# A two-layer graph attention kernel: layer 2's destination factors from broadcast rows on ScalarE instead of from products with stored masks

## The chip, the cores and the metric

The kernel runs on one core of a Trainium2 chip. The metric is the device time of one execution in microseconds. An execution taken by the profiler gives the profile and the trace; its own time stands beside its span.

## What is computed

The input is x (6250 nodes, 768 numbers each) and 100,000 edges from a source to a destination, sorted by destination; every node also has an edge to itself. In the reference, cut to what matters:

```python
def gat_conv(x, src, dst, W, a_src, a_dst, bias, heads):
    h = (x @ W).reshape(n, heads, -1)
    alpha_s = (h * a_src[None]).sum(-1)
    alpha_d = (h * a_dst[None]).sum(-1)
    e = leaky_relu(alpha_s[src] + alpha_d[dst], 0.2)
    e = exp(e - segment_max(e, dst)[dst])
    alpha = e / (segment_sum(e, dst)[dst] + 1e-16)
    return segment_sum(h[src] * alpha[:, :, None], dst).reshape(n, -1) + bias

h = maximum(layernorm(x), 0.0)
h = relu(gat_conv(h, src, dst, W1, a_src1, a_dst1, b1, heads=4))   # 4 x 64
h = relu(gat_conv(h, src, dst, W2, a_src2, a_dst2, b2, heads=1))   # 256
h = relu(h @ Wm1 + bm1)
out = x + (h @ Wm2 + bm2)
```

All of it is in float32.

## The kernel before

**Three stages.** The feature stage (from 0 to about 172 us in the trace) normalises x, multiplies with W1 and stores one row a node in a table in DRAM. Layer 1's edges run from there to about 1387, layer 2's from about 1442 (after a passage between the layers) to about 2560; the last node steps end at 2578.4.

**How the edges are tiled.** A tile is 128 edges. Two tiles are a pair, which is the unit of most instructions; a step `g` has two pairs (half-steps `2g` and `2g + 1`), a unit `u` has two steps (8 tiles, whose destinations lie near 64 nodes), and a block `t` has two units: 16 tiles and 128 nodes. There are 49 blocks, 98 units, 196 steps, 391 pairs and 782 tiles in a layer.

**What a tile goes through.** For each tile GpSimd (POOL) issues an indirect DMA (`gather`, L645) that brings the 128 source rows into a buffer `G`; 20 pair buffers go round. The softmax weight of an edge is exp(leaky(s + d)), with s from the source and d from the destination. Up to a factor that depends on the destination alone, which the division removes, it is max(exp(s), exp(0.2 s) rho) with rho = exp(-0.8 d). The rows of the table hold exp(s) and exp(0.2 s) (`powers`, L205). To bring rho to the edges, a mask (destination against partition, bf16, one per unit) is multiplied on TensorE with `win`, three bf16 parts of rho (`meet`, L691: 16 small products a block, into `e_ps`), and the parts are added (`join`, L699). In `pair`, VectorE takes the product and the maximum (L712, L715). For layer 1 it then scales the gathered rows (L724) and multiplies with a one-hot matrix `hot` (L673). For layer 2 it builds a weighted one-hot matrix `hw` of 128 x 128 instead, from `iota_ps`, the destination column and w (L719), which TensorE multiplies with the gathered rows (L736), summing in `o_ps`.

**Masks.** In layer 1, `make_mask` (L662) compares a broadcast row of destinations with the partition's number, and stores each mask to `mask_d` in DRAM (L664, 97 stores). In layer 2, `fetch_mask` (L617) brings them back (97 loads). Both go over SyncE's (SP's) DMA queue.

**Node steps.** When a unit's sum is done, VectorE adds it to the overlapping part of the unit before (`take_sum`, L753), ScalarE (ACT) copies quarters into place (L762), and each full block goes through its node steps. Those of layer 1 turn the block, apply relu (L918), multiply with W2, and write a row of the next table (L966 to L970). Those of layer 2 (`Node2.steps`) scale (L1066), turn (L912), relu (L918), multiply with Wm1 (L1075), relu (L1080), multiply with Wm2 (L1024, L1085), add x (L1089) and store.

**What sets the order.** The order on each engine is written out by hand (`manual_schedule`). Each engine works through its instructions in order, and waits on semaphores where data or a buffer isn't there. In layer 2, `UP_AT` says at which half-step a unit's sum is taken, and `STEPS_AT` at which half-steps a block's six node steps are placed: block t at 8t + 19 + 1, 2, 5, 8, 11 and 14. Gathers are placed eight steps (16 pairs) ahead of use.

**Between the layers.** `matched` prepares `win` and the own-edge weights (`prepare`, L557 to L594) and loads the weights of the last products. Some rows of layer 2's first tiles were gathered before all nodes were done, and are completed by products and an addition (`first_whole`, L303 and L305).

Of the kernel before, what the change touches and what calls it, by code (L numbers as in the profile page):

```python
# [10 lines left out]
F32 = mybir.dt.float32  # L11
# [42 lines left out]
SOON_AT = {2 * (8 * i + 11) + 1: i for i in range(len(SOON))}  # L54
SOON_FROM, SOON_HELD = min(SOON), 6
BARE = 8


UP_AT = {4 * u + 11: u for u in range(NU - 16)}
# [10 lines left out]
def kernel(  # L70
# [486 lines left out]
    def prepare(wk, layer, H):  # L557

        s, d = sd[layer][:, :, :H], sd[layer][:, :, H:]
        rho = wk.tile([P, NT, H], F32, name="rho")  # L560
        nc.scalar.activation(rho, d, AF.Exp, scale=SLOPE - 1.0)
        parts = wk.tile([P, NT, H, 3], BF16, name="parts")
        nc.vector.tensor_copy(parts[:, :, :, 0], rho)
        r1 = wk.tile([P, NT, H], F32, name="r1")
        nc.vector.tensor_sub(r1, rho, parts[:, :, :, 0])
        nc.vector.tensor_copy(parts[:, :, :, 1], r1)
        r2 = wk.tile([P, NT, H], F32, name="r2")
        nc.vector.tensor_sub(r2, r1, parts[:, :, :, 1])
        nc.vector.tensor_copy(parts[:, :, :, 2], r2)

        win = wk.tile([P, NG + 4, 3 * H], BF16, name="win")
        pv = parts.rearrange("p n h k -> p n (h k)").unsqueeze(2)
        for q in range(4):
            r = slice(32 * q, 32 * q + 32)
            to = win[r, q:q + NG].rearrange("p (n j) k -> p n j k", j=4)
            of = pv[r].to_broadcast([32, NT, 4, 3 * H])
            if q % 2:
                nc.scalar.activation(to, of, AF.Copy)
            else:
                nc.vector.tensor_copy(to, of)  # L580
        nc.vector.memset(win[64:96, 0:2], 0.0)
        nc.vector.memset(win[96:128, 0:3], 0.0)
        nc.vector.memset(win[0:32, NG:NG + 4], 0.0)
        e1 = wk.tile([P, NT, H], F32, name="e1")
        nc.scalar.activation(e1, s, AF.Exp)
        e2 = wk.tile([P, NT, H], F32, name="e2")
        nc.scalar.activation(e2, s, AF.Exp, scale=SLOPE)
        v = wk.tile([P, NT, H], F32, name="v")
        nc.vector.tensor_mul(v, e2, rho)
        own = wk.tile([P, NT, H], F32, name="own")  # L590
        nc.vector.tensor_max(own, v, e1)
        nc.vector.tensor_reduce(flags[:, layer - 1:layer], sd[layer].rearrange("p n k -> p (n k)"),
                                AX.X, ALU.max, apply_absolute_value=True)
        return SimpleNamespace(win=win, own=own)  # L594
# [14 lines left out]
            drow[r] = rowsp.tile([P, 16 * P], BF16, name="drow")  # L609
            nc.sync.dma_start(drow[r], bcast(dmod_d, 16 * P, r * 16 * P))  # L610

    def fetch_mask(u):

        if u < NU:
            b = (min(8 * u + 8, LAST) - 8 * u) * P
            mask[u] = maskp.tile([P, 8 * P], BF16, name="mask")
            nc.sync.dma_start(mask[u][:, :b], mask_d[u * P:(u + 1) * P, :b])  # L617

    def layer_edges(layer, H, node, pre, matched, pre_pool):

# [3 lines left out]
        with tc.tile_pool(name=f"eg{layer}", bufs=5) as eg, \  # L624
                tc.tile_pool(name=f"hw{layer}", bufs=10 if layer == 1 else 14) as hwp, \
                tc.tile_pool(name=f"sum{layer}", bufs=4) as sums, \
                tc.tile_pool(name=f"sm{layer}", bufs=4) as sm:
            G, hot, e_ps, o_ps = {}, {}, {}, {}

            def tiles(g):  # L630

# [33 lines left out]

            def make_hot(g):

# [14 lines left out]

            def meet(t):

                if t >= NT:
                    return
                e_ps[t] = ps.tile([P, 16, 6 * H], F32, name="e_ps", tag="e")
                for u, at, a, b in ranges(t):
                    m = mask.pop(u)
                    for k in range(a, b):  # L690
                        nc.tensor.matmul(e_ps[t][:, at + k, :3 * H], m[:, k * P:(k + 1) * P],  # L691
                                         pre.win[:, 2 * u + 2], start=True, stop=True)

            def join(t):
                if t >= NT:
                    return
                (_, _, a, _), (_, at, _, b) = ranges(t)
                T = slice(a, at + b)
                nc.vector.tensor_reduce(  # L699
                    e_ps[t][:, T, 3 * H:4 * H],  # L700
                    e_ps[t][:, T, :3 * H].rearrange("p t (h k) -> p t h k", k=3), AX.X, ALU.add)

            def pair(g, p):

                if 2 * p not in tiles(g):
                    return
                Gp = G.pop(TPG // 2 * g + p)
                e1, e2 = ((Gp[:, :, RW[1]:RW[1] + 4], Gp[:, :, RW[1] + 4:]) if layer == 1 else
                          (Gp[:, :, HID:HID + 1], Gp[:, :, HID + 2:]))
                at = TPG * (g % 4) + 2 * p  # L710
                rho, v, w = (e_ps[g // 4][:, at:at + 2, k * H:(k + 1) * H] for k in range(3, 6))
                nc.vector.tensor_mul(v, e2, rho)  # L712
# [14 lines left out]
                u = g // 2  # L727
                if u not in o_ps:
                    o_ps[u] = ps.tile([P, RW[layer]], F32, name="o_ps", tag="o", bufs=3)
                for t in range(2):  # L730
                    k = 2 * p + t
                    if layer == 2:
                        l, r = hw[:, t], Gp[:, t]
                    else:
                        l, r = hot[g][:, k], hw[:, t].rearrange("p h c -> p (h c)")
                    nc.tensor.matmul(o_ps[u], l, r[:, :RW[layer]], start=(g % 2 == 0 and k == 0),  # L736
                                     stop=(g % 2 == 1 and k == tiles(g)[-1]))
# [107 lines left out]
            for g in range(NG):  # L845
# [20 lines left out]
                if j == 0:  # L866
# [27 lines left out]
                if NG - 3 <= g < NG - 1:  # L894
                    stay_warm(3)
                hot.pop(g, None)
                if layer == 1 and g == NG - 6:
                    first_sources(2)
            if layer == 1:
                gather_up(NU - 1)  # L900
                advance(NG)
                stay_warm(4)
                for k in range(5):
                    fetch_mask(k)
            while late:
                advance(NG)
            at_end.clear()
# [14 lines left out]
    with tc.tile_pool(name="w2p", bufs=1) as wp, tc.tile_pool(name="wk2", bufs=2) as wk:  # L922
# [4 lines left out]
        class Node1:  # L927
# [17 lines left out]
            def steps(self, t, sum_, most=None, last=None):  # L945
# [32 lines left out]
    with tc.tile_pool(name="wmp", bufs=1) as wp, tc.tile_pool(name="x3", bufs=4) as xp, \  # L978
# [454 lines left out]
```

## Time and profile before

| | us |
|---|---|
| median of 3 runs | 2571.82 |
| lowest and highest | 2562.27, 2574.3 |
| the profiled execution | 2580.24 |
| its span | 2578.4 |

| engine | busy, us | share of the span | instructions |
|---|---|---|---|
| PE (TensorE products) | 1809.2 | 70% | 7727 |
| PEld (TensorE weight loads) | 1288.6 | 50% | 7729 |
| DVE (VectorE) | 1397.1 | 54% | 4195 |
| ACT (ScalarE) | 409.4 | 16% | 1273 |
| POOL (GpSimd) | 1523.6 | 59% | 1666 |

The mean clock granted to TensorE was 0.802 of full speed. The page's lines name engine, line of the kernel, what is written and read, how many, busy time and mean duration, and the idle time of the engine just before, with what ended it. "issue" is idle time in which the engine waited for nothing that the profile shows; "remote" is a release by something the trace doesn't name. A float32 product shows as two records, each with a weight load.

### The profile page before, as it was taken

To read this page: it belongs to the slowest core of one execution; us is meant where nothing else is said; L and a number is where in the kernel's file an instruction comes from. 1 tells how busy PE (TensorE), PEld (TensorE's weight loads), DVE (VectorE), ACT (ScalarE), POOL (GpSimd) and SP (SyncE) were. 2 spreads that over 40 slices of the span, in tenths; PEclk is the share of its full clock that TensorE was granted. 3 is DMA by queue.
4 is the path that set the end of the run, shared out by engine and by line. 5 is a ranking of instruction groups with operands and counts; after the bars stand their busy time and mean duration, and the time that the engine had idled before them with its cause. 6 is when DMAs were issued, how large, how long until landed. Compare 5 with 4: busy or idle time off the path is not lost.

```text
span 2578.4 us, 26497 instructions
## 1 busy us (share of the span) xinstructions
PE 1809.2 (70%) x7727; PEld 1288.6 (50%) x7729; DVE 1397.1 (54%) x4195; ACT 409.4 (16%) x1273; POOL 1523.6 (59%) x1666
## 2 busy tenths in 40 slices
PE   9944768867767777677675656676766766777677
PEld 7732546646545555555553434454444444454455
DVE  7733666666666676576565443444444444444444
ACT  6730011111111111111111011111111111111111
POOL 5366555565655655565554566666666666666661
PEclk9975878878878888887888768777778778877778
DMA  9994444545544544454434434445554555444442
GB/s 351 358 329 114 143 140 137 147 137 147 149 141 143 154 143 143 143 149 138 142 107 125 126 113 152 146 140 152 153 150 136 151 152 156 151 136 145 148 147 76
DMA packets 167328, 400.37 MB, mean 155 GB/s; under 512 B 36631, under 2 KB 54254, under 8 KB 167174
## 3 DMA queue, kind: packets, MB, share of 16 engines
q0 software_dynamic: 75072, 211.10, 29.9%
q1 hardware_dynamic: 90732, 185.99, 21.0%
q10 hardware_dynamic: 1370, 1.48, 0.2%
q8 instruction: 65, 1.06, 0.2%
q14 instruction: 89, 0.73, 0.1%
HBM read 333.87 MB, written 64.56 MB: 155 GB/s over the span
## 4 chain that ended last, share of the span: by engine, by line
PE 30%; issue 22%; DVE 21%; another core or an unknown queue 16%; POOL 4%; DMA 3%; ACT 1%; SPq 0%; DVEq 0%; POOLq 0%; ACTq 0%
PE o_ps L736 17%; PE y_ps L1085 4%; DVE hw L724 4%; POOL G L645 4%; DVE hot L673 4%; PE missing L389 3%; PE h_ps L447 3%; DVE e_ps L722 2%; DVE e_ps L712 2%; DVE hw L719 2%; DMA G<-table,src_i 2%; DVE acc L753 2%; DVE mask L662 1%; PE tp L1075 1%
## 5 line engine op out<-in xcount | busy, mean ns | idle before, releaser
L645 POOL DMA_INDIRECT G<-table,src_i x1507 | 1431.5, 950 | 874.1 <-issue 377.3
L736 PE MATMUL o_ps<-G,hw 128*128 128x258 f32 x1564 | 524.6, 463 | 225.5 <-issue 196.2
L736 PE MATMUL o_ps<-hw,hot 128*128 128x260 f32 x1564 | 504.6, 463 | 207.6 <-issue 128.8
L736 PEld LDWEIGHTS o_ps<-G,hw 128*128 128x128 f32 x1564 | 353.0, 232 | 368.8 <-issue 272.0
L736 PEld LDWEIGHTS o_ps<-hw,hot 128*128 128x128 f32 x1564 | 337.8, 227 | 347.2 <-issue 169.0
L762 ACT ACTIVATE sum<-acc 32x260 f32<-32x260 f32 (+1 forms) x384 | 160.0, 417 | 1421.8 <-DVE hw L724 631.8
L719 DVE TENSOR_SCALAR hw<-iota_ps,dcol,w 128x128 f32<-128x128 f32 x782 | 285.0, 406 | 15.4 <-DVE w L715 0.6
L724 DVE TENSOR_TENSOR hw<-G,e_ps 128x520 f32<-128x520 f32 x391 | 271.8, 695 | 22.5 <-DVE e_ps L722 6.3
L389 PE MATMUL missing<-kept,soon_hit 128*128 128x268 f32 x1028 | 251.4, 398 | 35.2 <-issue 35.2
L379 DVE TENSOR_TENSOR soon_hit<-soon_of,iota_ps 128x1408 f32<-128x1408 int32 (+18 forms) x46 | 75.6, 1643 | 323.2 <-remote 258.8
L389 PEld LDWEIGHTS missing<-kept,soon_hit 128*128 128x128 f32 x1028 | 196.3, 195 | 75.2 <-issue 41.4
L1089 DVE TENSOR_TENSOR y<-y_ps,xt 128x384 f32<-128x384 f32 (+1 forms) x98 | 54.6, 557 | 289.8 <-PE o_ps L736 106.8
L1085 PE MATMUL y_ps<-wm,mT 128*128 128x384 f32 x392 | 182.0, 594 | 18.2 <-issue 15.5
L691 PE MATMUL e_ps<-win,mask 128*128 128x12 bf16 (+1 forms) x1564 | 72.0, 168 | 130.9 <-issue 122.6
L447 PE MATMUL h_ps<-w,r 128*128 128x264 f32 (+1 forms) x588 | 139.3, 390 | 9.6 <-ACT r L437 5.0
L691 PEld LDWEIGHTS <-mask 128*128 128x128 bf16 x1564 | 65.0, 100 | 148.0 <-issue 140.3
L673 DVE TENSOR_TENSOR hot<-iota_ps,dcol 128x512 f32<-128x512 f32 x196 | 133.6, 682 | 2.3 <-remote 2.3
L712 DVE TENSOR_TENSOR e_ps<-G,e_ps 128x8 f32<-128x8 f32 (+1 forms) x782 | 125.5, 160 | 5.2 <-issue 0.9
L1085 PEld LDWEIGHTS y_ps<-wm,mT 128*128 128x128 f32 x392 | 77.4, 219 | 98.4 <-issue 65.5
L447 PEld LDWEIGHTS h_ps<-w,r 128*128 128x128 f32 x588 | 108.8, 192 | 32.6 <-issue 7.2
L1080 ACT ACTIVATE mT<-tp,bm1c 128x128 f32<-128x128 f32 x98 | 30.6, 363 | 507.8 <-remote 235.1
L753 DVE SCALAR_TENSOR_TENSOR acc<-acc,keep,o_ps 128x260 f32<-128x260 f32 (+1 forms) x192 | 91.6, 477 | 14.3 <-PE o_ps L736 10.2
(415 smaller groups left out, 1246.8 us busy)
## 6 DMA issues: line engine op xcount, KB each, us to landing
xt<-in_x SPq DMA_DIRECT2D x96, 384.0 KB
drow<-dmod_d SPq DMA_DIRECT2D x49, 512.0 KB
mask_d<-mask SPq DMA_DIRECT2D x97, 256.0 KB
mask<-mask_d SPq DMA_DIRECT2D x97, 256.0 KB
G<-table,src_i POOLq DMA_INDIRECT x1507
xTt<-in_xT SPq DMA_DIRECT2D x49, 384.0 KB
out<-y SPq DMA_DIRECT2D x48, 384.0 KB
table<-kept SPq DMA_DIRECT2D x49, 134.0 KB
```

What stands on the lines that cost most here:

```text
L389: nc.tensor.matmul(soon_p[k], hit[:, T - there], kept[T], start=(T == there), stop=(T == NT - 1))
L447: nc.tensor.matmul(h_ps[:, :n], r[:, k], w1[:, k, :n], start=(k == 0), stop=(k == KI - 1))
L645: nc.gpsimd.indirect_dma_start(out=G[k // 2][:, k % 2], out_offset=None, in_=table[layer], in_offset=bass.IndirectOffsetOnAxis(ap=src_i[:, ...
L673: nc.vector.tensor_tensor(hot[g][:, T[0]:T[0] + n], iota_ps.unsqueeze(1).to_broadcast([P, n, P]), dcol[:, k:k + n].unsqueeze(2).to_broadca ...
L691: nc.tensor.matmul(e_ps[t][:, at + k, :3 * H], m[:, k * P:(k + 1) * P], pre.win[:, 2 * u + 2], start=True, stop=True)
L712: nc.vector.tensor_mul(v, e2, rho)
L719: nc.vector.tensor_scalar(hw[:, t], iota_ps, dcol[:, k:k + 1], w[:, t], ALU.is_equal, ALU.mult)
L724: nc.vector.tensor_mul(hw, Gp[:, :, :RW[1]].rearrange("p t (h c) -> p t h c", h=H), w.unsqueeze(3).to_broadcast([P, 2, H, C + 1]))
L736: nc.tensor.matmul(o_ps[u], l, r[:, :RW[layer]], start=(g % 2 == 0 and k == 0), stop=(g % 2 == 1 and k == tiles(g)[-1]))
L753: nc.vector.scalar_tensor_tensor(acc, run[0], keep[:, u % 2:u % 2 + 1], o_ps.pop(u), ALU.mult, ALU.add)
L762: nc.scalar.activation(done[t][r], acc[r], AF.Copy)
L1085: nc.tensor.matmul(y_ps, mT[:, j], wm2[:, j, s * half:(s + 1) * half], start=False, stop=(j == KH - 1))
```

## The change

Layer 2 no longer uses masks and products for its destination factors. The rows of layer 2's table hold s and -0.8 s instead of powers. `slopes` makes, for each unit, a row of 128 numbers -0.8 d, one for each destination of its window: copies on ScalarE, one transpose on TensorE, a copy, and a store to `slope_d`. It is called once in layer 1 at step 150 for units 0 to 55, and once at the start of layer 2 for the rest. `fetch_slopes` brings the rows of eight units at a time to all 128 partitions (up to 512 KB each, 13 loads on SP's queue, two buffers). In `pair`, ScalarE computes for each tile Relu(row - 0.8 s) and then Exp(that + s), each over 128 x 128 with a bias from the gathered row; VectorE's product and maximum of layer 2 go, and `hw` becomes (iota == destination) times this 128 x 128 weight. Layer 1 keeps its masks, products and joins, but no longer stores the masks. `prepare` no longer makes `win` for layer 2. The scratch for the descriptors of POOL's DMAs is halved.

```diff
+SLOPES, SLOPES_AT = 56, 150
...
-    mask_d = dram.tile([NU * P, 8 * P], BF16, name="mask_d")
+    slope_d = dram.tile([NU, P], F32, name="slope_d")
...
+        win = None
+        if layer == 1:
+            parts = wk.tile([P, NT, H, 3], BF16, name="parts")
...
-    def fetch_mask(u):
-
-        if u < NU:
-            b = (min(8 * u + 8, LAST) - 8 * u) * P
-            mask[u] = maskp.tile([P, 8 * P], BF16, name="mask")
-            nc.sync.dma_start(mask[u][:, :b], mask_d[u * P:(u + 1) * P, :b])
+    def slopes(pool, a, b):
+
+        n = b - a
+        rr = pool.tile([P, n + 2], F32, name=f"slope{a}")
+        nc.vector.memset(rr, 0.0)
+        for q, first, past in ((0, 0, 1), (1, 0, 0), (2, 0, 0), (3, -1, 0)):
+            lo, hi = max(a // 2 + first, 0), min(b // 2 + past, NT)
+            at = 2 * lo + (-1, 0, 0, 1)[q] - a + 1
+            r = slice(32 * q, 32 * q + 32)
+            nc.scalar.activation(rr[r, at:at + 2 * (hi - lo)].rearrange("p (n k) -> p n k", k=2),
+                                 sd[2][r, lo:hi, 1:2].to_broadcast([32, hi - lo, 2]), AF.Copy,
+                                 scale=SLOPE - 1.0)
+        p = ps.tile([P, P], F32, name="slope_ps", tag="e")
+        nc.tensor.transpose(p[:n], rr[:, 1:n + 1], ident)
+        turned = pool.tile([P, P], F32, name=f"slopeT{a}")
+        nc.scalar.activation(turned[:n], p[:n], AF.Copy)
+        nc.sync.dma_start(slope_d[a:b], turned[:n])
...
+            def fetch_slopes(k):
+
+                if layer == 2 and k * 8 < NU:
+                    n = min(8, NU - 8 * k) * P
+                    slope[k] = eg.tile([P, 8 * P], F32, name="slope", bufs=2)
+                    nc.sync.dma_start(slope[k][:, :n], bcast(slope_d, n, k * 8 * P))
...
                 if layer == 2:
-                    return fetch_mask(u + 1)
+                    return
...
-                nc.sync.dma_start(mask_d[u * P:(u + 1) * P, a:b], mask[u][:, a:b])
...
-                if t >= NT:
+                if t >= NT or layer == 2:
                     return
                 e_ps[t] = ps.tile([P, 16, 6 * H], F32, name="e_ps", tag="e")
...
                 if layer == 2:
-                    w = sm.tile([P, 2, H], F32, name="w")
-                    nc.vector.tensor_max(w, v, e1)
+                    u = g // 2
+                    rows = slope[u // 8][:, u % 8 * P:(u % 8 + 1) * P]
+                    w = sm.tile([P, 2, P], F32, name="w")
+                    for t in range(2):
+                        nc.scalar.activation(w[:, t], rows, AF.Relu, bias=Gp[:, t, HID + 2:])
+                    for t in range(2):
+                        nc.scalar.activation(w[:, t], w[:, t], AF.Exp, bias=Gp[:, t, HID:HID + 1])
                     hw = hwp.tile([P, 2, P], F32, name="hw")
                     for t in range(2):
                         k = TPG * g + 2 * p + t
-                        nc.vector.tensor_scalar(hw[:, t], iota_ps, dcol[:, k:k + 1], w[:, t],
-                                                ALU.is_equal, ALU.mult)
+                        nc.vector.scalar_tensor_tensor(hw[:, t], iota_ps, dcol[:, k:k + 1], w[:, t],
+                                                       ALU.is_equal, ALU.mult)
...
+            fetch_slopes(0)
             matched()
...
                     meet(t + 1)
+                    if t % 4 == 1:
+                        fetch_slopes(t // 4 + 1)
...
+                if layer == 1 and g == SLOPES_AT:
+                    slopes(pre_pool, 0, SLOPES)
...
-                for k in range(5):
-                    fetch_mask(k)
...
-                nc.scalar.activation(row[:, :HID], h_ps[:, :HID], AF.Copy)
-                powers(row[:, HID:HID + 1], row[:, HID + 2:], h_ps[:, HID:HID + 1])
+                nc.scalar.activation(row[:, :HID + 1], h_ps[:, :HID + 1], AF.Copy)
+                nc.scalar.activation(row[:, HID + 2:], h_ps[:, HID:HID + 1], AF.Copy, scale=SLOPE - 1.0)
...
+            slopes(pre, SLOPES, NU)
             vars(pre2).update(vars(prepare(pre, 2, 1)))
...
-                   dynamic_dma_scratch_size=8192)
+                   dynamic_dma_scratch_size=4096)
```

More of the change, by code (lines that the diff above doesn't have):

```diff
@@ L561, in prepare @@
         nc.scalar.activation(rho, d, AF.Exp, scale=SLOPE - 1.0)
[L562 to L583, printed above, removed]
+        win = None
+        if layer == 1:
+            parts = wk.tile([P, NT, H, 3], BF16, name="parts")
+            nc.vector.tensor_copy(parts[:, :, :, 0], rho)
+            r1 = wk.tile([P, NT, H], F32, name="r1")
+            nc.vector.tensor_sub(r1, rho, parts[:, :, :, 0])
+            nc.vector.tensor_copy(parts[:, :, :, 1], r1)
+            r2 = wk.tile([P, NT, H], F32, name="r2")
+            nc.vector.tensor_sub(r2, r1, parts[:, :, :, 1])
+            nc.vector.tensor_copy(parts[:, :, :, 2], r2)
+            win = wk.tile([P, NG + 4, 3 * H], BF16, name="win")
+            pv = parts.rearrange("p n h k -> p n (h k)").unsqueeze(2)
+            for q in range(4):
+                r = slice(32 * q, 32 * q + 32)
+                to = win[r, q:q + NG].rearrange("p (n j) k -> p n j k", j=4)
+                of = pv[r].to_broadcast([32, NT, 4, 3 * H])
+                if q % 2:
+                    nc.scalar.activation(to, of, AF.Copy)
+                else:
+                    nc.vector.tensor_copy(to, of)
+            nc.vector.memset(win[64:96, 0:2], 0.0)
+            nc.vector.memset(win[96:128, 0:3], 0.0)
+            nc.vector.memset(win[0:32, NG:NG + 4], 0.0)
         e1 = wk.tile([P, NT, H], F32, name="e1")
@@ L610, in fetch_rows @@
             nc.sync.dma_start(drow[r], bcast(dmod_d, 16 * P, r * 16 * P))
-    def fetch_mask(u):
-        if u < NU:
-            b = (min(8 * u + 8, LAST) - 8 * u) * P
-            mask[u] = maskp.tile([P, 8 * P], BF16, name="mask")
-            nc.sync.dma_start(mask[u][:, :b], mask_d[u * P:(u + 1) * P, :b])
+    def slopes(pool, a, b):
[5 more added lines that the diff above has]
+            at = 2 * lo + (-1, 0, 0, 1)[q] - a + 1
+            r = slice(32 * q, 32 * q + 32)
+            nc.scalar.activation(rr[r, at:at + 2 * (hi - lo)].rearrange("p (n k) -> p n k", k=2),
[6 more added lines that the diff above has]
+        nc.sync.dma_start(slope_d[a:b], turned[:n])
     def layer_edges(layer, H, node, pre, matched, pre_pool):
@@ L627, in layer_edges @@
                 tc.tile_pool(name=f"sm{layer}", bufs=4) as sm:
-            G, hot, e_ps, o_ps = {}, {}, {}, {}
+            G, hot, e_ps, o_ps, slope = {}, {}, {}, {}, {}
+            def fetch_slopes(k):
[3 more added lines that the diff above has]
+                    nc.sync.dma_start(slope[k][:, :n], bcast(slope_d, n, k * 8 * P))
             def tiles(g):
@@ L694, in join @@
             def join(t):
-                if t >= NT:
+                if t >= NT or layer == 2:
                     return
@@ L707, in pair @@
                 Gp = G.pop(TPG // 2 * g + p)
[L708 to L712, printed above, removed]
-                if layer == 2:
-                    w = sm.tile([P, 2, H], F32, name="w")
-                    nc.vector.tensor_max(w, v, e1)
+                if layer == 2:
+                    u = g // 2
[5 more added lines that the diff above has]
+                        nc.scalar.activation(w[:, t], w[:, t], AF.Exp, bias=Gp[:, t, HID:HID + 1])
                     hw = hwp.tile([P, 2, P], F32, name="hw")
@@ L718, in pair @@
                         k = TPG * g + 2 * p + t
-                        nc.vector.tensor_scalar(hw[:, t], iota_ps, dcol[:, k:k + 1], w[:, t],
-                                                ALU.is_equal, ALU.mult)
-                else:
+                        nc.vector.scalar_tensor_tensor(hw[:, t], iota_ps, dcol[:, k:k + 1], w[:, t],
+                                                       ALU.is_equal, ALU.mult)
+                else:
+                    e1, e2 = Gp[:, :, RW[1]:RW[1] + 4], Gp[:, :, RW[1] + 4:]
+                    at = TPG * (g % 4) + 2 * p
+                    rho, v, w = (e_ps[g // 4][:, at:at + 2, k * H:(k + 1) * H] for k in range(3, 6))
+                    nc.vector.tensor_mul(v, e2, rho)
                     nc.vector.tensor_max(w, v, e1)
```

## The prediction

> **What bounds the kernel now.** The whole page first: the shares of the engines, and the chain that ended last.
>
> ```profile
> PE 1809.2 (70%) x7727; PEld 1288.6 (50%) x7729; DVE 1397.1 (54%) x4195; ACT 409.4 (16%) x1273; POOL 1523.6 (59%) x1666
> ...
> PE 30%; issue 22%; DVE 21%; another core or an unknown queue 16%; POOL 4%; DMA 3%; ACT 1%; SPq 0%; DVEq 0%; POOLq 0%; ACTq 0%
> ```
>
> No engine is full, and a fifth of the chain is "issue", where the engine waits for nothing that the profile shows. ACT is at 16%. Averages hide stages, so next comes the table of busy time by stretch (us, then PE, PEld, DVE, ACT, POOL with their counts, granted clock, DMA share, GB/s). Layer 2's edges run from 1442 to about 2560.
>
> ```profile
> 1600.00:1800.00 200.00, 136.50 (x555) 91.69 (x555) 84.13 (x319) 29.34 (x77) 129.05 (x136) 0.75 0.48 143
> 1800.00:2000.00 200.00, 138.74 (x597) 95.05 (x597) 90.05 (x342) 28.83 (x76) 131.29 (x138) 0.77 0.49 146
> 2000.00:2200.00 200.00, 141.30 (x566) 91.58 (x566) 88.08 (x334) 29.39 (x77) 129.25 (x136) 0.77 0.50 149
> ```
>
> PE is busiest, at about 70%, and POOL's gathers come next; DVE is at 44%, ACT at 15%, DMA at half. Layer 2 takes (2560 - 1442) / 49 = 22.8 us for each block of 128 nodes (16 tiles of 128 edges, 8 pairs). Now the waits between 1500 and 2400 (total us, times, longest).
>
> ```profile
> PEld o_ps L736 <- issue: 238.7, 216, 2.7
> ACT mT L1080 <- remote: 210.0, 16, 19.3
> PE o_ps L736 <- issue: 169.7, 166, 2.7
> ...
> POOL G L645 <- issue: 157.2, 515, 0.6
> ...
> POOL G L645 <- remote: 72.2, 37, 3.7
> POOL G L645 <- PE o_ps L736: 61.1, 46, 3.6
> ```
>
> PE's edge product loses 170 us to "issue", not to a gather or a weight. POOL does wait for PE, some 3.6 us at a time: its ring of 20 pair buffers is full, and it goes on when PE frees a pair. So PE sets the pace of layer 2 and POOL follows. How close is POOL? Its order of time, from 1988:
>
> ```profile
> 1988.30 0.95 POOL L645 DMA_INDIRECT G<-table,src_i  x1 [0.30 <-issue]
> 1989.55 0.94 POOL L645 DMA_INDIRECT G<-table,src_i  x1 [0.30 <-issue]
> ...
> 1998.28 0.94 POOL L645 DMA_INDIRECT G<-table,src_i  x1 [0.30 <-issue]
> 2001.93 0.94 POOL L645 DMA_INDIRECT G<-table,src_i  x1 [2.71 <-remote]
> ```
>
> Unhindered it issues one gather per 1.25 us (0.95 and 0.30), which is 16 x 1.25 = 20.0 us a block: only 2.8 us below the 22.8. Last, PE in order of time around one run of the small products:
>
> ```profile
> 2035.74 1.90 PE L736 MATMUL o_ps<-G,hw 128*128 128x258 f32 x8
> 2037.48 1.05 PE L1075 MATMUL tp<-rT,wm 128*128 128x128 f32 x8
> 2038.37 0.54 PE L691 MATMUL e_ps<-win,mask 128*128 128x3 bf16 x16
> 2038.77 0.68 PE L736 MATMUL o_ps<-G,hw 128*128 128x258 f32 x2
> 2039.94 0.46 PE L736 MATMUL o_ps<-G,hw 128*128 128x258 f32 x1 [0.49 <-issue]
> 2042.04 0.38 PE L736 MATMUL o_ps<-G,hw 128*128 128x258 f32 x1 [1.64 <-issue]
> 2042.78 0.38 PE L736 MATMUL o_ps<-G,hw 128*128 128x258 f32 x1 [0.36 <-issue]
> ```
>
> Undisturbed, eight records (four tiles) take 1.74 us from start to start. Right after the 16 products of L691 PE falls into a halting stretch: single records 0.7 to 2 us apart with nothing waited for, about 12 us here (to 2052), and at the half clock afterwards. Undisturbed a block would need 16 x 0.435 = 7.0 for the edges, 2 x 1.66 for y, 0.9 and 0.2 for the two other products and 0.4 for L691: 11.8 us. The other 11 of the 22.8 us are halts and half clock. In order of time, most of these stretches in layer 2 begin within 2 us of an L691 run. None is seen from 0 to 172 us, where there is no L691, nor from 1344 to 1442, nor after 2494, when the last mask transfers leave SP's queue (one at 2500). Two of the last L691 runs (2509, 2533) are followed by none, so masks may matter rather than the products.
>
> **What the skill says.** "TensorE: Matmul & The Clock Gate", Part 1: the clock is either half or full, by activity in a window of about 3.4 us. The trace agrees: clock 0.75 to 0.77 as a mean, the same products at 0.22 or 0.46 us a record. "DMA: Bandwidth & Descriptors", Anatomy of one DMA (SWDGE): about 2.0 us fixed for a transfer started by POOL; here gathers land 2.1 to 2.3 us after issue, some 45 us ahead of use. "ScalarE: Activation LUTs", What ACT_TABLE_LOAD costs: 280 ns + 0.833 ns a column with a pointer bias, and neighbours overlap by about 93 ns. The trace agrees: L420 (one column, pointer bias, SBUF) 282 ns.
>
> **The change, part by part.**
> 1. Products with masks in layer 2 (784 of L691), and join (49 x 0.21 us of DVE), go. Between 1450 and 2400, 41 blocks, L691 is busy 27.0 us with 23.7 idle before it: 1.2 us a block. If halts belong to it or to its masks, up to 11 us a block go; but from 2.8 us on POOL is late, so that this is the most that a block gives in the long run.
> 2. The mask stores of layer 1 (97) and fetches of layer 2 (97 of 256 KB) leave SP's queue. Bounds: nothing (DMA is half used) to the halts of layer 1, about 340 us by adding them up in its order of time. I take nothing for layer 1, whose products stay.
> 3. DVE per pair: 0.157 (L712) and 0.160 (L715) go; the two hw instructions change from 406 ns to a two-tensor form. Nearest row: L753, 477 ns for 258 columns; less 130 columns at 1.05 ns (L1007: 784 columns in 976 ns; L1089: 384 in 557) gives 0.34; I take 0.34 to 0.41. DVE falls to about 8 us a block beside POOL's 20: worth nothing by itself.
> 4. ACT gains four 128-column instructions a pair, 1564 in all. From L420: 282 + 127 x 0.833 = 388 ns each, the pitch 0.29 to 0.39. A block: 32 x 0.29 to 0.39 = 9.4 to 12.4, plus now 29 us in 200 = 3.3: 13 to 16 us, under 20. The worst bound, L1066's 509 ns for 256 columns, would give 19.6. The hiding work is POOL's; without it 32 x 0.39 would bound. No table load is expected: L109's one serves Exp and Relu already.
> 5. A new order: ACT now stands between gather and hw. In its queue w of the next pair lies behind rT, mT, o and sum. mT waits for PE's m_ps of three half-steps before, so w is at most three pairs ahead. From m_ps to the hw needed: mT 0.62, w 1.5, hw 0.7, 2.8 us; PE's three pairs at POOL's pace are 7.5 us. Nothing; at PE's full pace (2.6) it would be tight. A gather's buffer is now held for ACT too, which is done with it before PE.
> 6. Slope rows: ACT copies, one transpose and a store twice; at step 150 the inputs are some six blocks old, at layer 2's start they cost 2 to 3 us, against 3 us of DVE and 1.4 of ACT (L578) that prepare loses. Zero net, under the fixes of L305, which hold the first pair until 1441.5. Slope fetches: 13 of 512 KB on SP against 97 of 256 KB; first needed long after issue. Rows with raw s instead of powers: one small ACT instruction fewer a block.
> 7. The smaller ring for descriptors: two to four gathers are in flight at 1.25 us and 2.3 us landing. Zero, at worst a new wait on POOL, which then counts fully.
>
> **The sum.** If the halts go with L691 and masks, POOL sets layer 2. In the trace 40 gathers of its 771 are started before 1456; the ring frees at 1444.4, and 741 more steps of 1.2547 us (its mean where it doesn't wait) end at 2374. Behind the last: landing 2.3, weights and last products about 2.5, and the last node steps, 15.5 from 2563 to 2578.4: 20 us. Span 2394. With the 1.84 around it 2396, against 2580.2 for the profiled execution; that stood 0.33% above the median of 2571.8, so 2388. I add 12 for waits of POOL while PE still catches up: 2400, a gain of 172.
>
> **Rivals.**
> - PE still halts, by time or by number of instructions. For it: layer 1's stretches don't always begin at L691. Against: the undisturbed end. Then only L691's own time goes: 1.2 to 2 us a block, 60 to 100 us: 2474 to 2514; say 2485.
> - Layer 1 gains as well, because mask traffic causes the halts: a third of its 340 us more, 2400 - 110 = 2290. For it: the stretches end with the masks. Against: one stretch a block, two masks.
> - ACT becomes the bound: slower. Place: the four instructions ahead of every hw. It decides from (22.8 - 3.3) / 32 = 0.61 us each with their waits; at 0.7, 25.7 us a block give 49 x 2.9 = 142 more: 2714. For it: ACT is strictly in order and w waits behind mT, whose waits reach 19 us now. Against: 0.39.
> - No change: another hidden limit, as the POOL wait of part 7, takes the 2.8 us: 2570.
>
> **Chances.** POOL-bound 0.50; halts stay 0.27; layer 1 too 0.07; ACT 0.11; no change 0.05. A difference of 0.5% is about what a measurement of this kernel can tell from none. Faster 0.84, same 0.05, slower 0.11. The range 2370 to 2560 leaves out ACT and layer 1, and takes in the bounds of the unknown costs.
>
> **What would show it.** Right: POOL's gathers at 1.25 us with hardly a wait for PE; PE waiting for DMA or hw; clock and "issue" changed in layer 2; layer 1 within 1% in length; ACT at some 15 us a block. Wrong: "issue" ahead of L736's successor undiminished; POOL still waiting for PE or now for ACT; ACT instructions of 0.6 us or more; layer 1 shorter.

## The result, and the profile after

| | before | after |
|---|---|---|
| median of 19 runs each, us | 2568.38 | 2582.47 |
| lowest and highest | 2562.27, 2575.78 | 2568.23, 2590.17 |
| the profiled execution | 2580.24 | 2584.67 |
| its span | 2578.4 | 2582.9 |

The ratio is 1.0055, with a 95% interval of 1.0043 to 1.0066: 14 us slower, where 172 us faster was forecast. The experiments ran in five groups, each beside the kernel before; in three of them (those of b_lean, a_narrow2 and a_copy2 below) the kernel before took 2099.8 to 2104.4 us instead of 2566.8 to 2591.0, no trace of those groups shows PE halting, and since what makes the difference was not found, every run is compared with before in its own group only.

The page of the changed kernel, its engines and its chain:

```profile
PE 1720.1 (67%) x6948; PEld 1236.2 (48%) x6949; DVE 1243.6 (48%) x3356; ACT 866.0 (34%) x2796; POOL 1524.2 (59%) x1666
...
another core or an unknown queue 6%; ACT 6%; PE 5%; DVE 2%; issue 2%; POOL 0%; DMA 0%
...
L739 DVE SCALAR_TENSOR_TENSOR hw<-iota_ps,dcol,w 128x128 f32<-128x128 f32 x782 | 245.4, 349 | 448.4 <-ACT w L735 291.5
...
L733 ACT ACTIVATE w<-slope,G 128x128 f32<-128x128 f32 x782 | 266.8, 389 | 48.6 <-issue 39.9
```

PE lost 89 us of work and DVE 153, ACT gained 457. POOL is as it was. The shares of the chain add up to a fifth only: the trace could not follow it. The table of busy time by stretch (columns as before):

```profile
1600.00:1800.00 200.00, 123.19 (x424) 82.79 (x423) 60.39 (x184) 108.12 (x348) 128.95 (x137) 0.78 0.44 130
1800.00:2000.00 200.00, 120.27 (x456) 84.83 (x454) 60.23 (x184) 108.90 (x351) 131.92 (x139) 0.81 0.45 129
2000.00:2200.00 200.00, 129.39 (x456) 85.21 (x456) 64.76 (x196) 110.42 (x355) 129.10 (x137) 0.81 0.46 134
```

PE's busy time was 136 to 141 us in 200 before and is some 124 now, and the number of gathers is the same 137. Work left the engines and the pace did not change: from the starts of the edge product, 40 blocks apart, a block takes 23.54 us before and 23.40 after. (The count starts at the fifth block. Started up to three blocks earlier or later it gives 23.33 to 23.56 before and 23.39 to 23.82 after, so the two don't differ.) Layer 1's last edge product starts at 1383.6 and 1383.5, and layer 2's first one at 1443.0 and 1442.3. The waits of the changed kernel between 1500 and 2400 (us, times, longest):

```profile
ACT mT L1108 <- remote: 251.0, 29, 21.3
PEld o_ps L760 <- DVE hw L739: 250.3, 44, 25.8
DVE y L1117 <- remote: 234.2, 25, 12.3
PE o_ps L760 <- DVE hw L739: 231.9, 29, 25.7
DVE hw L739 <- ACT w L735: 219.2, 89, 14.2
POOL G L666 <- issue: 146.1, 424, 3.6
POOL G L666 <- ACT mT L1108: 101.2, 29, 4.5
```

PE's "issue" is gone from the head of the list. In its place PE waits some 8 us at a time for hw, DVE waits 10 us at a time for "remote" before it adds x, and ACT for "remote" before mT. One block, on PE, then DVE, then POOL, in order of time:

```profile
2011.89 1.56 PE L1113 MATMUL y_ps<-wm,mT 128*128 128x384 f32 x4
2013.29 1.90 PE L760 MATMUL o_ps<-G,hw 128*128 128x258 f32 x8
2015.03 1.05 PE L1103 MATMUL tp<-rT,wm 128*128 128x128 f32 x8
2015.92 1.04 PE L760 MATMUL o_ps<-G,hw 128*128 128x258 f32 x4
2025.87 3.81 PE L760 MATMUL o_ps<-G,hw 128*128 128x258 f32 x8 [8.91 <-DMA G<-table,src_i]
```

```profile
2014.31 0.64 DVE L739 SCALAR_TENSOR_TENSOR hw<-iota_ps,dcol,w 128x128 f32<-128x128 f32 x2 [1.03 <-ACT w L733]
2024.99 0.56 DVE L1117 TENSOR_TENSOR y<-y_ps,xt 128x384 f32<-128x384 f32 x1 [10.04 <-remote]
2025.47 0.86 DVE L739 SCALAR_TENSOR_TENSOR hw<-iota_ps,dcol,w 128x128 f32<-128x128 f32 x3
```

```profile
2022.00 0.95 POOL L666 DMA_INDIRECT G<-table,src_i  x1 [0.30 <-issue]
2023.25 0.95 POOL L666 DMA_INDIRECT G<-table,src_i  x1 [0.30 <-issue]
2027.88 0.94 POOL L666 DMA_INDIRECT G<-table,src_i  x1 [3.68 <-ACT mT L1108]
```

DVE's second addition of y needs PE's products of L1113 and the loaded x. The products ran from 2011.89 to about 2013.4 (the ends of PE's records are modelled), and PE went on through 20 further records. The addition started only at 2024.99. The trace's own record of PE's signals (the semaphore updates by which other engines learn that a product is done; the trace has 1240 of PE's 1518) says why: none between 2016.56 and 2024.97, one more at 2027.11, and then seven in 0.35 us. By its records PE had done the work, but its signals came some 11 us late. All that waits for PE then waits: DVE's addition, hw behind it, mT, and PE itself for hw. (At 2025.87 the profile names a DMA as what PE waited for, but the hw that PE needs ended only at 2025.8.) POOL meanwhile goes on, until it has no free buffer, at 2024.20. I call this a hold.

Two more counts from the trace say what is late. Of the 75 additions of y between 1500 and 2400, 30 begin more than 2 us after both PE's products and DVE's own work before them were over; 29 of these begin 0.02 us after a signal of PE, so they don't wait for x. The signals of the other engines are hardly ever late: of 610 tiles in the same stretch, hw begins more than 0.5 us after its w and DVE's own work before it in 4, and PE's product never more than 0.06 us after its hw and PE's own work before it. In the profile before, the halting stretch that the prediction shows from 2039 to 2052 has the same signature: PE signals at 2041.33, 2044.17 and 2047.00, then nothing until 2054.12, then ten signals in 0.47 us. I take the halts before and the late signals after for the same thing.

### The profile page after: what moved, and what is told of

Same layout as the page of the kernel before. It is cut to its first block, busy times and chain, and to the rows that moved or that the text cites. A ratio compares the mean times of both kernels' runs of the same rounds, so it can differ in the third digit from the quotient of the medians.

```text
span 2582.9 us, 24782 instructions
## 1 busy us (share of the span) xinstructions
PE 1720.1 (67%) x6948; PEld 1236.2 (48%) x6949; DVE 1243.6 (48%) x3356; ACT 866.0 (34%) x2796; POOL 1524.2 (59%) x1666
## 5 line engine op out<-in xcount | busy, mean ns | idle before, releaser
L760 PE MATMUL o_ps<-G,hw 128*128 128x258 f32 x1564 | 471.2, 445 | 313.3 <-DVE hw L739 272.5
L760 PE MATMUL o_ps<-hw,hot 128*128 128x260 f32 x1564 | 496.5, 456 | 192.9 <-issue 125.2
L760 PEld LDWEIGHTS o_ps<-G,hw 128*128 128x128 f32 x1564 | 330.5, 222 | 429.4 <-DVE hw L739 300.7
L739 DVE SCALAR_TENSOR_TENSOR hw<-iota_ps,dcol,w 128x128 f32<-128x128 f32 x782 | 245.4, 349 | 448.4 <-ACT w L735 291.5
L733 ACT ACTIVATE w<-slope,G 128x128 f32<-128x128 f32 x782 | 266.8, 389 | 48.6 <-issue 39.9
L735 ACT ACTIVATE w<-w,G 128x128 f32<-128x128 f32 x782 | 268.3, 388 | 27.1 <-remote 9.8
L1113 PE MATMUL y_ps<-wm,mT 128*128 128x384 f32 x392 | 179.9, 588 | 60.9 <-ACT mT L1108 60.9
L1113 PEld LDWEIGHTS y_ps<-wm,mT 128*128 128x128 f32 x392 | 78.6, 223 | 127.5 <-ACT mT L1108 64.6
L711 PE MATMUL e_ps<-win,mask 128*128 128x12 bf16 x782 | 38.0, 170 | 84.3 <-issue 82.8
L945 ACT ACTIVATE rT<-tp,bT 128x128 f32<-128x128 f32 x196 | 60.5, 359 | 99.5 <-remote 73.0
```

Source lines behind the costliest of these rows:

```text
L733: nc.scalar.activation(w[:, t], rows, AF.Relu, bias=Gp[:, t, HID + 2:])
L735: nc.scalar.activation(w[:, t], w[:, t], AF.Exp, bias=Gp[:, t, HID:HID + 1])
L739: nc.vector.scalar_tensor_tensor(hw[:, t], iota_ps, dcol[:, k:k + 1], w[:, t], ALU.is_equal, ALU.mult)
L1113: nc.tensor.matmul(y_ps, mT[:, j], wm2[:, j, s * half:(s + 1) * half], start=False, stop=(j == KH - 1))
```

## Experiments

Theory 1: PE's signals are held while POOL's gathers follow each other, and a block is POOL's run and its pause. Theory 2, which is nearer to the prediction: the halts are PE's own, or belong to the products and masks. "Block" is the mean of 40 blocks of layer 2 from the starts of the edge product, from the fifth block on.

**Half of the gathers (a_half, b_half).** In both kernels layer 2 gathers the first tile of a pair only, and uses its rows twice.

```diff
-                    if soon or k < FIRST + len(THERE.get(layer, ())):
+                    if soon or k < FIRST + len(THERE.get(layer, ())) or (layer == 2 and k % 2):
```

> The changed kernel, where layer 2 gathers only the first tile of each pair and uses its rows for both tiles; the output is not the reference's. Theory 1 (the pace of a block is POOL's run of 16 gathers and a pause, and PE's signals come late only while gathers follow each other): a block falls from 23.3 us to what ACT and PE need, 13 to 15 us, so the time falls by some 49 x 9 = 440 us to about 2140, and the silent stretches of PE go. Theory 2 (PE halts by itself some 9 us a block, whatever POOL does): a block is PE's 11.4 us and 9, so 20.4, the time about 2440.

> The kernel before, with the same halving of layer 2's gathers; the output is not the reference's. Theory 1: a block falls from 22.8 us to some 13 us (PE 11.8, DVE 8 pairs of 1.1 and the node steps), about 2100 us. Theory 2 (halts of PE that belong to the small products, the masks or PE itself): the block keeps its 22.8 us, since POOL did not set it, and the time stays within 1% of 2570.

Measured: a_half 2132.25 us, ratio 0.8226 (0.8187 to 0.8265), block 13.80; b_half 2055.87 us, ratio 0.7927 (0.7889 to 0.7966), block 12.21. Busy time by stretch, b_half, then a_half:

```profile
1500.00:1700.00 200.00, 200.00 (x1115) 150.46 (x1115) 169.23 (x650) 56.86 (x150) 125.34 (x133) 1.00 0.63 199
1700.00:1900.00 200.00, 199.78 (x1133) 151.04 (x1132) 170.49 (x644) 56.72 (x149) 127.30 (x132) 1.00 0.65 198
```

```profile
1500.00:1700.00 200.00, 190.82 (x759) 120.75 (x757) 107.85 (x325) 183.01 (x600) 111.39 (x118) 1.00 0.48 145
1700.00:1900.00 200.00, 190.70 (x762) 121.55 (x763) 106.61 (x319) 182.97 (x599) 110.35 (x117) 1.00 0.48 145
```

b_half has all 782 products with masks of layer 2 and all mask loads, and PE is full, at full clock, without a halt between 1500 and 1900; the same execution shows halts in layer 1, whose gathers are all there. So the halts belong neither to the products nor to PE's work alone: they go with the gathers. With half of the gathers the kernel before is bound by PE (200 of 200 us), the changed one by ACT (183 of 200), and is the slower by 1.6 us a block. Theory 1 had said about 2140 and 2100 us, theory 2 2440 us and no change. Theory 2 and the prediction's step fall.

It is not the rate of the gathers or of the bytes: b_half has 133 gathers in 200 us, as the kernel before has 136, and moves 199 GB/s instead of 146. What differs is how many follow each other. Counted between 1500 and 2400 (2000 for the two halves) as gathers without a break of over 0.6 us, the runs are mostly of 10 to 16 gathers in the kernel before, of at most 8 in b_half and of at most 5 in a_half; the additions of y come up to 10.0, 3.6 and 0 us late. So b_half is not free of late signals: 16 of its 84 additions begin over 1 us late, and PE's signals still come in bunches 0.04 us apart. They are short enough that PE, which is full, loses nothing by them.

**The removal alone (b_lean, b_lean2).** The kernel before without layer 2's products, joins, mask loads, and without the mask stores; nothing takes their place.

```diff
                 if layer == 2:
-                    return fetch_mask(u + 1)
+                    return
...
-                nc.sync.dma_start(mask_d[u * P:(u + 1) * P, a:b], mask[u][:, a:b])
...
-                if t >= NT:
+                if t >= NT or layer == 2:
                     return
                 e_ps[t] = ps.tile([P, 16, 6 * H], F32, name="e_ps", tag="e")
...
+                    rho, v = ones_c.unsqueeze(1).to_broadcast([P, 2, 1]), sm.tile([P, 2, H], F32, name="v")
```

> The kernel before without layer 2's products with masks, joins and mask loads, and without layer 1's mask stores; the destination factor in layer 2 is the constant 1, so the output is not the reference's. Nothing is added in their place. The prediction's step (the halts belong to these products or masks): a block falls to POOL's 20.0 us, the time to about 2400. Theory 1 (a block is POOL's run of 16 gathers at 1.25 us and a pause of some 3.5 us, whatever PE has to do): the time stays within 0.7% of before, POOL's pauses and PE's silent stretches stay.

> The kernel before without layer 2's products with masks, joins, mask loads and layer 1's mask stores (destination factor 1, so not the reference's output), once more. On a chip with holds: within 0.7% of before, since the block is POOL's run and its pause, not PE's work; about 2400 us if the halts belong to what is removed. On a chip without: 0.2% faster, as measured there.

b_lean: ratio 0.9983 (0.9975 to 0.9991), in a group without holds, so that it doesn't decide between the two. b_lean2: 2560.83 us, ratio 0.9969 (0.9956 to 0.9982), with holds, block 23.10. One stretch of b_lean2 and its waits between 1500 and 2400:

```profile
1800.00:2000.00 200.00, 128.41 (x447) 88.14 (x448) 91.56 (x342) 30.25 (x79) 132.99 (x139) 0.80 0.44 128
```

```profile
DVE y L1089 <- remote: 273.6, 28, 13.3
...
POOL G L645 <- issue: 164.2, 536, 0.7
...
PEld o_ps L738 <- issue: 100.1, 44, 8.8
```

All that the change removes is worth 6 us, not 170. POOL has 139 gathers in 200 us, as before. The holds are there without the products and masks of layer 2, in the shape of the changed kernel: DVE waits for "remote" 10 us at a time.

**Both kernels again (b_copy, a_copy, a_8192).** a_8192 is the changed kernel with the larger scratch and 11 buffers for hw; b_4096 is the kernel before with the smaller scratch.

```diff
-                   dynamic_dma_scratch_size=4096)
+                   dynamic_dma_scratch_size=8192)
```

> The kernel before, unaltered, for its trace on this chip: same time as before. Where it takes about 2104 us: blocks of 20.0 us with POOL never waiting, and no halting stretch after the small products L691, though they and the mask loads are all there. If the halts belonged to the products or to the masks, they would be there on every chip.

> The changed kernel, unaltered. On a chip where the kernel before takes about 2580 us (PE's signals are held while gathers run): again 0.3 to 0.8% slower than before. On a chip where it takes about 2104 us (no holds): both kernels have POOL's 16 x 1.25 = 20.0 us a block, so within 0.3% of before; if the removed products or masks had cost anything there, it would be faster by more than that.

> The changed kernel with the scratch for POOL's descriptors as large as before (8192), and 11 instead of 14 buffers for hw so that it fits. If the smaller ring is part of the loss: some 5 us less than the changed kernel. If not: the same within 0.2%.

> The kernel before with the halved scratch for POOL's descriptors and nothing else of the change. If the ring costs nothing, the time stays within 0.3% of before; if it is what makes the changed kernel slower, it is about 14 us longer.

b_copy 1.0003 (0.9988 to 1.0017); a_copy 1.0053 (1.0031 to 1.0074); a_8192 1.0056 (1.0037 to 1.0075); b_4096, in another group, 1.0021 (1.0006 to 1.0035). The loss repeats. With the larger ring the changed kernel takes the same time (2582.10 against 2581.93 us), but a_8192 has fewer buffers for hw too, which was not tested alone. In the kernel before the smaller ring costs 7 us (2 to 9 by the interval), within the 0.3% that its expectation put as nothing. b_copy fell in a group with holds, so it did not show what its expectation asked.

**The changed kernel without holds (a_copy2).**

> The changed kernel, unaltered, if possible in a group without holds, where the kernel before takes 2103 us: POOL's 20.0 us a block bounds both, ACT's 13.8 us stays under it and the stretch after the last gather is short, so within 0.3% of before (b_lean, which only leaves work out, was 0.2% faster there). If ACT's chain adds to each block, it is slower by more. In a group with holds: 0.5% slower again.

Measured: 2101.36 us beside 2099.80, ratio 1.0006 (0.9997 to 1.0014): no difference, as expected. Block 20.07. Busy time by stretch and waits between 1200 and 2000:

```profile
1200.00:1400.00 200.00, 150.16 (x531) 98.33 (x530) 73.87 (x221) 133.06 (x412) 151.25 (x161) 0.85 0.51 151
1400.00:1600.00 200.00, 145.10 (x513) 94.32 (x512) 72.49 (x218) 131.94 (x409) 151.27 (x161) 0.85 0.51 154
...
1800.00:2000.00 200.00, 147.99 (x540) 95.64 (x538) 73.74 (x220) 133.28 (x413) 151.48 (x160) 0.88 0.50 149
```

```profile
DVE hw L739 <- ACT w L735: 503.9, 280, 5.5
...
ACT w L733 <- DMA G<-table,src_i: 216.6, 248, 4.1
...
POOL G L666 <- issue: 73.7, 242, 0.3
```

160 to 161 gathers in 200 us are one per 1.25 us: POOL never waits longer than 0.3 us, and everybody else waits for gathers (ACT for G, DVE for ACT, PE for DVE). No addition of y comes late here, though POOL's gathers never break off: gathers one after another are not enough for a hold. POOL's 20.0 us a block bound the kernel before as well there: b_lean, which is that kernel with work left out, has a block of 20.04 and gains 0.17%. The clock stands at 0.85 to 0.88, with PE busy 145 to 150 us of 200; it was 1.00 in b_half.

**Fewer gathers, breaks, narrower rows, more ACT work.** a_three leaves out every fourth gather; a_break puts two memsets of 400 columns on POOL after every eighth; a_narrow gathers 131 numbers of a row; a_act2 does each Relu of w twice; a_pace puts one memset of 64 columns after each gather. The edit of a_break:

```diff
+                    if layer == 2 and k % 8 == 7:
+                        for _ in range(2):
+                            nc.gpsimd.memset(pause, 0.0)
```

> The changed kernel with three gathers for every four tiles of layer 2 (the fourth tile uses the rows of the third; the output is not the reference's). POOL needs 12 x 1.25 = 15.0 us a block, ACT 13.8. Theory 1, with a hold as soon as gathers follow each other without a break: 15.0 and a pause of 2 to 3.5 us, so 17 to 18.5 us a block, about 2290 us. If the hold belongs to a fixed period instead, the block stays at 23.4. If there is a hold only in runs that are longer than these, 15.0 us a block, about 2170.

> The changed kernel, where layer 2's gathers bring 131 numbers of a row instead of 259 (from a second table of half rows, stored in layer 1 beside the first), and the product reads 129 columns twice, so that PE, ACT and DVE do what they did; the output is not the reference's. POOL issues the same 16 gathers a block. If it is the issue of gathers that holds PE's signals: block 23.4 us as before, the time unchanged. If it is the bytes that they move: no hold, 20.0 us a block, about 2400.

> The changed kernel with two memsets of 400 columns on POOL after every eighth gather in layer 2: two breaks of about 1 us a block. If a short break is enough to let PE's signals through: 20.0 + 2 = 22 us a block instead of 23.4, about 60 us faster. If the signals come only when POOL has run out of buffers: the pause takes what is left of its 3.5 us, the block stays at 23.4 (or grows by up to 2 us, 100 us slower).

> The changed kernel with each Relu of w done twice, so 16 more instructions of 0.29 us pitch a block on ACT (4.7 us, 18.5 instead of 13.8 a block). If ACT's part in the loss is only the stretch after the last gather, where 2.5 blocks are worked off at ACT's pace: 2.5 x 4.7 = 12 us over the changed kernel. If ACT also lengthens every block (it has to work off what a hold kept back): up to 49 x 4.7 = 230 us more.

> The changed kernel with one small memset on POOL after each gather of layer 2, which slows POOL's run by its length, x us a gather. Theory 1: a block is 16 (1.25 + x) us and the pause of about 3.5, so that the time grows by 771 x (0.1 us gives 77). Theory 2: POOL has 2.8 to 3.5 us of room a block; up to x = 0.2 nothing changes.

The first three were run a second time (a_narrow a third), to meet a group with holds:

> The changed kernel with three gathers for four tiles in layer 2 (output not the reference's), in a group where the kernel before takes about 2570 us. POOL needs 15.0 us a block, ACT 13.8. If holds come with any unbroken run of gathers: 17 to 18.5 us a block, about 2290. If they need runs with more than 92% of POOL's time: 15.0, about 2170.

> The changed kernel with gathers of 131 numbers a row instead of 259 in layer 2, as in the run before on half rows (output not the reference's), in a group where the kernel before takes about 2570 us. If the issue of gathers holds PE's signals: block 23.4 us, time within 0.7% of the changed kernel. If it is the bytes: block 20.0 us, about 2410. Where the kernel before takes 2104 us, this run repeats the other one.

> The changed kernel with two breaks of about 1 us a block on POOL, in a group where the kernel before takes about 2570 us. Breaks that let the signals through: 22.0 us a block, about 2510. Breaks that only take the place of the pause: 23.4, about 2580. Breaks that add: 25.4, about 2680.

> The changed kernel with half rows in layer 2's gathers (output not the reference's), once more. Both groups that held it were free of holds. If that is chance, this group may be of either kind; where the kernel before takes about 2570 us, it tells bytes (about 2410) from issue (about 2580).

| run | ratio to before in its group | block, us |
|---|---|---|
| a_three, a_three2 | 0.8882, 0.8881 | 15.07, 15.07 |
| a_narrow, a_narrow2, a_narrow3 | 0.9991, 0.9994, 0.9997 | 20.01, 20.02, 20.01 |
| a_break, a_break2 | 1.0446, 1.0435 | 22.01, 22.01 |
| a_act2 | 1.0204 (1.0188 to 1.0220) | 20.74 |
| a_pace (group with holds) | 1.0062 (1.0049 to 1.0076) | 24.35 |

None but a_pace met holds. So they say nothing on them, but much on the bound without them: the block is the number of gathers times 1.25 us (12 make 15.07, 16 make 20.0), it grows by what a break adds (two times 0.94 us make it 22.01), and half of the bytes change nothing (20.01). a_act2 is the point where ACT takes over: 20.74 us a block and 69 us from the last gather to the end, against 25.9 for a_copy2. That is 43 us over the kernel before, where its expectation had 12 or up to 230. One stretch of a_act2:

```profile
1400.00:1600.00 200.00, 139.96 (x507) 86.77 (x507) 71.55 (x214) 184.18 (x556) 151.25 (x161) 0.95 0.52 151
```

POOL still issues its 161 gathers, so the 20 pair buffers take up what ACT falls behind, and the loss shows after the last gather. All three groups that held a_narrow, and only these, were without holds; with five groups that may be chance.

a_pace is a miss for theory 1. Its 24.35 us a block is no contradiction to its time: the count gives 23.58 to 24.05 when it starts up to three blocks earlier or later. POOL's step grew from 1.251 to 1.284 us, so theory 1 as a sum (run and a fixed pause) asked for 771 x 0.033 = 25 us over the changed kernel; 1.0062 against its 1.0053 to 1.0055 is 2 us. POOL's waiting in layer 2 (its steps beyond their median, summed) fell from 171 to 153 us: the pause gave way. That is what theory 2 had said of this run; it fell by b_half. So under holds a block is not simply POOL's run plus a constant, and what a block is made of there was not found.

## Why the prediction was wrong, step by step

- **The step that failed** is the first of the sum: "If the halts go with L691 and masks, POOL sets layer 2". They do not go with them, and the 2.8 us a block that this term gave is not there. b_lean2 takes products and masks out and gains 6 us; b_half keeps them and PE doesn't halt; the changed kernel has neither and is held 10 us a block. The products came right after L1075 in PE's order, where a hold showed first as starts that came late, and the order of time was read as cause.
- **The evidence of the end was misread.** "None after 2494" is true of PE's starts only. PE's signals in the trace before are silent from 2498.9 to 2504.6 and from 2514.9 to 2522.2, and six or more then come 0.04 to 0.09 us apart. A hold shows in starts only when PE has enough to start; the waits for "remote" (ACT mT, 210 us) were in the list, and were passed over.
- **What sets the pace** was put the wrong way round. That POOL waits for a buffer from PE, up to 3.6 us at a time, was taken to mean that PE is the bound and POOL the next one. Half of the gathers take 48% off each block of the kernel before (23.5 to 12.2): the length of a block goes with the gathers, not with PE's work. Where there are no holds, POOL bounds both kernels outright. Where there are, PE's signals come when POOL has stopped: between 1500 and 2400, 55 of 59 bunches of them in the kernel before and 63 of 64 in the changed one begin while POOL waits in a break of over 0.6 us, and such breaks are a sixth of the time. POOL in turn goes on when signals come, so this alone doesn't show which of the two makes the other wait; that half of the gathers frees PE does.
- **Right:** POOL at 1.25 us a gather and 20.0 us a block, once nothing holds PE (20.07); the new ACT instructions, 388 and 389 ns for an estimate of 388 (the formula of the Trainium skill, "ScalarE: Activation LUTs", What ACT_TABLE_LOAD costs, gives 387); four of them in 1.17 us; ACT's 13 to 16 us a block (13.8 in a_half); hw at 349 ns for 340 to 410; nothing for layer 1 and for the passage between the layers.
- **Small misreadings** that don't bear on the result: layer 2 has 782 of the products L691, not 784; its gathers land 2.4 to 2.5 us after issue (the median), not 2.1 to 2.3; and a block by the starts of the edge product is 23.5 us, not 22.8, so that POOL's 20.0 lies 3.5 below it. The ring, put at zero, is not quite that in the kernel before (7 us).
- **The rivals.** "No change: another hidden limit", at 0.05, comes nearest (2570 against 2582 us), but not by the limit that it names as an example, a new wait of the smaller ring. "PE still halts" had the halts right and expected 60 to 100 us from L691's own time; it is 6, since PE's work does not set the block. ACT as the bound was not reached, but it is near: half as many instructions for w again (a_act2) reach it.
- **The 14 us.** Part is settled. After the last gather some 2.5 blocks are worked off without holds. At ACT's 13.8 instead of PE's 12.2 us that is 4.0 us by estimate, and the traces have 54.8, 53.7 and 53.9 us from the last gather to the end for the changed kernel (a_8192 the last) against 52.1 and 49.3, so 3.4. The rest, some 11 us, lies before the last gather, and is not settled. The smaller ring may have a part in it: it costs the kernel before 7 us, but the changed kernel doesn't gain from the larger one. Traces can't tell: POOL's waiting in layer 2 of the kernel before differs by 17 us between two executions (170 and 154). Without holds the difference is 1.6 us, within its interval.

No version that computes the reference's result was faster than the kernel before. What the runs point to is fewer gathers or shorter runs of them; that was not tried with a result that is the reference's.

## What to carry to other kernels

Where one engine idles for "issue" or "remote" and another pauses for it once a period, neither reading ("PE is the bound", "POOL is the next") is safe: take half of one engine's work away, even if the result is then no longer the reference's, and see whose pace changes. Being beside each other in time, even most of the times, is not cause when both recur once a block; compare starts with the signals that others receive. Before a gain is forecast from removed work, ask which single engine's count times step comes nearest to the period (here POOL's 16 x 1.25 = 20.0 us of 23.5), and what is left of the gain if that engine and its waits stay as they are. A mean over 40 blocks still depends on which 40: here by 0.2 to 0.8 us in the traces with holds.

## What the runs showed that was not expected

- PE's signals can come 11 us after the work, once a block, while gathers are issued one after another; most of the silent times before they come lie near multiples of 0.70 us (5.6, 6.3, 7.0, 7.7, 8.4), the step at which PE's single instructions crept in the kernel before, and the rest then comes at 0.04 us each. In a_half, whose gathers break off after 5 at most, no addition of y was late; in b_half, after 8 at most, by 3.6 us at most. What holds them was not found.
- The same kernels, unchanged, ran at 2100 to 2104 us in some groups and at 2567 to 2591 in others. Layer 1 is part of it: its last edge product starts at 1102.2 us in a_copy2 and at 1383.5 in a_copy. Two of the groups, those of b_lean and b_lean2, ran on one and the same chip, the first without holds and the second with them, so the chip alone does not decide it, as the expectations of b_copy and a_copy had assumed.
- An unhindered PE at full clock worked off a block of the kernel before in 12.2 us (b_half); 11.8 had been added up from single rows.
